# A two-layer graph network on one core: sums of h on GpSimd, aggregates that end bank by bank, and rows put on all partitions by DMA

## The chip, the core and the metric

The kernel runs on one core of a Trainium2 chip. The core has five engines with a queue of instructions each, which run side by side and wait for each other through semaphores: TensorE (PE in the profile, with PEld for its weight loads), VectorE (DVE), ScalarE (ACT), GpSimd (POOL) and SyncE (SP, which here only issues DMAs). Sixteen DMA engines move data between DRAM and the on-chip memory (SBUF). TensorE writes its results to PSUM, eight banks of 128 partitions x 512 f32 values. An instruction of an engine starts only when the one before it in its queue has started, so a wait holds up all that stands behind it.

The metric is the device time of one launch in microseconds, the median of several runs. Before the change it is 3184.61 us (seven runs, 3182.16 to 3187.07).

## What is computed

There are N = 2708 nodes with 1024 features each and a 0/1 matrix adj of 2708 x 2708. Each of two layers normalizes the rows, applies a ReLU, attends over adj and adds the result to x:

```python
# layer 0
h = jnp.maximum(_layernorm(x), 0.0)
f = h @ Wf + bf
g = h @ Wg + bg
e = relu(f @ g.T)
attention = softmax(where(adj > 0, e, -9e15), axis=1)
x = x + attention @ (h @ W + bW)
# layer 1
h = jnp.maximum(_layernorm(x), 0.0)
hW = h @ W1
e = leaky_relu(hW @ a1 + (hW @ a2).T, 0.2)
attention = softmax(where(adj > 0, e, -9e15), axis=1)
x = x + relu(attention @ hW)
```

All is f32.

## The kernel before

**Panels.** The nodes whose attention is computed are cut into five panels p = 0 to 4, with 576, 576, 532, 512 and 512 columns. Within a panel everything is kept transposed: the nodes attended to lie on the partitions, in tiles of 128, and the panel's own nodes lie along the free dimension. There are 20 full tiles, taken as ten pairs q = 0 to 9, and a leftover unit (a tile MONO of 128 nodes and one TINY of 20).

**Seven products.** Each large matrix product is made by Strassen's scheme in Winograd's form: M1 to M7, seven half-size products instead of eight, on sums and differences of the blocks. The sums of the left side (of h, of the weights) are made once, written to DRAM and loaded again for each panel: hs_d holds the blocks of transposed h for the scores, hg_d[layer] the blocks of h for the aggregates, md_d and wt_d the weights' blocks.

**Stages.** First the product M of the weights Wf and Wg is made, while `make_pairs` reads x by pairs, normalizes it, transposes it on TensorE (tile h_ps), makes the sums for the scores on VectorE (`sums`, tile hsT) and stores them to hs_d. Then, for layer 0 and each panel: `project_q` (q), `scores` (ten rounds, one for each pair, each with seven products, tile names sx, sy, sz; the left operands As are loaded from hs_d), a softmax whose steps are spread over later products, `aggregate` (tiles gx, gy, gz, gv; left operands hc loaded from hg_d), and `project` (px, py, pz, pv). For layer 1 and each panel: `weights1` (attention weights from the two scores of each node), `aggregate`, and `project`.

**Order.** A scheduler orders the instructions of each engine and gives the tiles their buffers. The loads on SP's queue keep the order of the program (`load`); stores go through POOL's queue (`store`). Two pools matter: `slots`, 54 buffers of 576 columns, and `strm` (called the stream pool here), 12 buffers of 1024 columns, for all tiles loaded or stored in transit: wg, wf, hsT, As, adj_i, hr, md, hc, hl, w. A load whose buffer isn't free waits on SP, and the loads behind it wait too. Small pieces of work are put into a list by `put` and run between products by `behind`.

**What the change touches.**

- `rows_h` and `sums_h` (the sums of h for layer 0's aggregates). `rows_h` stores the four blocks of each pair as they are to hg_d[0]. After all pairs are made, `sums_h` loads them again, two tiles hr of 512 KB for each pair, makes four operations on VectorE and stores the three places M6 and M7, M3, M5. These pieces run during the scores of panel 0; `sums_until_all` runs what is left ahead of the aggregate's second product.
- `pair_h` does the same from the tiles in SBUF. Before, only layer 1 uses it, on VectorE.
- `accumulate` with `by_k` (the aggregates). The ten pairs are the steps k, and d runs over the four PSUM banks of a product. Before, all steps run k by k with the four banks inside, so the banks end together; then the leftover unit's products (`left_over`, loaded as hl) are added for some products, and the four banks are evicted.
- `spread` puts a column of values (one per partition) on all partitions as a row: a transpose on TensorE for each tile (sp_ps) and a copy out of PSUM. It is used for r in `scores` (rb), for the softmax's maxima (mb), and for z and none in `weights1` (ub, vb). `take_shifts` and `take_weights` run inside the aggregate of the panel before, after its products M3 and M7.

Of the kernel before, what the change touches and what calls it, by code (L numbers as in the profile page):

```python
# [8 lines left out]
FP = mybir.dt.float32  # L9
# [48 lines left out]
def kernel(  # L58
# [69 lines left out]
    def stream(name, shape=(P, D), dt=FP):  # L128
        return strm.tile(list(shape), dt, tag="strm", name=name)
# [7 lines left out]
    def load(o, i):  # L137
        for a, b in in_16(o, i):
            tc.keep_in_program_order(nc.sync.dma_start(a, b))  # L139

    def store(o, i):
        for a, b in in_16(o, i):
            nc.gpsimd.dma_start(a, b)  # L143
# [16 lines left out]
    md_d = dram.tile([P, 7, NH, W], FP, name="md_d")  # L160
    wt_d = [dram.tile([P, 4, NH, W], FP, name=f"wt{l}_d") for l in range(2)]
    mk_d = [dram.tile([P, NQ + 1, 2, width[p]], BF, name=f"mk_d{p}") for p in range(NP)]
    x1_d = [dram.tile([P if t < TINY else NY, D], FP, name=f"x1_d{t}") for t in range(NT)]

    ident = consts.tile([P, P], FP, name="ident")
# [63 lines left out]
    def spread(o, cols):  # L229

        at = 0
        for g in range(0, len(cols), 4):
# [6 lines left out]
            copy(o[:, at:at + w], ps[:, :w])  # L239
            at += w  # L240

    def add(o, a, b):
        nc.vector.tensor_tensor(o, a, b, OP.add)

    def sub(o, a, b):
        nc.vector.tensor_tensor(o, a, b, OP.subtract)
# [42 lines left out]
    def left_h(l, hm, ht):  # L289

        for e in range(2):
            store(hgl_d[l][:, e, :W], hm[e])
            for d in range(NH):
                g = slice(B32 * d, B32 * (d + 1))
                store(hgl_d[l][g, e, W:], ht[e][g, d * P:(d + 1) * P])

    def pair_h(l, q, ha, hb):

        n = P
        on = nc.vector  # L300
# [12 lines left out]
    def rows_h(q, ha, hb):  # L313

        i, j = group_of[q]
        for m, h in ((M1, ha[0]), (M5, ha[1]), (M2, hb[0]), (M4, hb[1])):
            store(hg_d[0][i][:, m, j], h)

    summed = [0]

    def sums_h():

        def fetch(q, two):
            i, j = group_of[q]
            for m in (M1, M2):
                two.append(stream("hr", (P, 2, W)))
                load(two[-1], hg_d[0][i][:, m:m + 2, j])

        def first(q, two):
            (a0, a1), (b0, b1) = ((t[:, 0], t[:, 1]) for t in two)  # L330
            add(b1, a1, b1)
            sub(a1, a0, a1)

        def second(q, two):
            (a0, a1), (b0, b1) = ((t[:, 0], t[:, 1]) for t in two)
            sub(a0, b1, a0)
            sub(b0, b0, a0)
            i, j = group_of[q]
            store(hg_d[0][i][:, M6:M7 + 1, j], two[0])
            store(hg_d[0][i][:, M3, j], b0)  # L340
            store(hg_d[0][i][:, M5, j], b1)
            summed[0] += 1
        for q in range(NQ):
            two = []
            put(1.4, lambda q=q, two=two: first(q, two), lambda q=q, two=two: fetch(q, two))
            put(1.4, lambda q=q, two=two: second(q, two))

    u = consts.tile([P, NC], FP, name="u")
    v = consts.tile([P, NC], FP, name="v")
# [5 lines left out]
    def make_pairs():  # L355
# [6 lines left out]
                load_rows_of(t, xs[q][-1], x)  # L362

        def rows(q):
            left_h(0, *xs[q]) if q == LEFT else rows_h(q, *xs[q])

        def turned(q, k, e):
            t = units[q][k]
# [68 lines left out]
        for i, q in enumerate(todo):  # L437
# [7 lines left out]
            if i == 1:  # L445
                put_dots(todo[0])
                put_dots(todo[1])
        sums_h()

    def make_until(q):  # L450
        while min(q, NQ - 1) not in made:
# [119 lines left out]
        picks.append(t)  # L571


    def accumulate(left, right, K, h, order, then, evict, name, prepare={}, rate=0.0, by_k=False, more={}, room=()):

        acc = {}
        at = {M1: "x", M2: "x", M5: "y", M3: "y", M6: "z", M7: "z", M4: "v" if by_k else "z"}
        for m in order:  # L580
            start = at[m] not in acc
            if start:
                acc[at[m]] = [bank(f"{name}{at[m]}{d}") for d in range(NH)]
            ps = [t[:, :h] for t in acc[at[m]]]
            for k, d in ([(k, d) for k in range(K) for d in range(NH)] if by_k else
                         [(k, d) for d in range(NH) for k in range(K)]):
                nc.tensor.matmul(ps[d], left(m, k, d), right(m, k), start=(start and k == 0),  # L587
                                 stop=(k == K - 1 and m not in more), skip_group_check=True)
                if by_k and d == NH - 1 and k % 3 == 2:
                    behind(rate)  # L590
                if by_k and d == NH - 1 and k == K // 2 and (m, k) in more:
                    more[m, k]()
                if not by_k and k == K - 1:
                    evict[m](d, ps[d])
                    behind(rate, m in room)
            if by_k:
                if m in more:
                    more[m](ps)
                for d in range(NH):
                    evict[m](d, ps[d])  # L600
# [193 lines left out]

    exps, LAG = [0], 2

    def sums_until_all():
        while summed[0] < NQ:
            one()

    def exps_until(n):
        while exps[0] < n:
            one()
# [8 lines left out]
    def aggregate(l, p, S, sm, then={}, rate=3.0):  # L812
# [33 lines left out]
        def left_over(ps, e, s, start=False):  # L846


            two = stream("hl", (P, W + P))
            load(two, hgl_d[l][:, e])  # L850
            for d in range(NH):
                nc.tensor.matmul(ps[d], two[:, d * P:(d + 1) * P], S[MONO][:, s], start=start, stop=False,
                                 skip_group_check=True)
            for d in range(NH):
                g = slice(B32 * d, B32 * d + NY)
                nc.tensor.matmul(ps[d], two[g, W:], S[TINY][g, s], start=False, stop=True, skip_group_check=True)  # L856

        def into_m15():
            ps = [bank(f"gw{d}")[:, :h] for d in range(NH)]
# [219 lines left out]
    def scores(p, B):  # L1079
# [3 lines left out]
        lo, hi = slice(0, h), slice(h, w)  # L1083
        fetch, convert, turn = makers[p]
        rb = slot("rb")
        spread(rb, columns_of(p, r_[:, first_col[p]:]))
        acc = slot("acc")
        S = [None] * NT
        rates = (0.6, 1.0, 0.65, 0.65, 0.65)
# [285 lines left out]
    for p in range(NP):  # L1375
        got["S"], got["acc"] = scores(p, B)
        generated[p] = NQ + 1
        ahead[0] = 2
        S = got["S"]
        hooks = {M1: lambda p=p: take_max(p), M2: lambda p=p: take_softmax(p)}  # L1380
        if p + 1 < NP:
            B = project_q(p + 1, hooks)
        else:
            nc.hold = ("vector",)
            project(0, p - 1, G.pop(p - 1), finish0(p - 1), hooks)
            nc.hold = ()
            scores_before()
        then = {M5: prepare_W} if p == 0 else {}
        if p == 0:
            then[M1] = sums_until_all  # L1390
        if p == NP - 2:
            then[M2] = lambda: first_masks(NP - 1, 0)
            then[M6] = lambda: first_masks(NP - 1, 1)
            then[M7] = lambda: first_masks(NP - 1, 2)
        G[p] = aggregate(0, p, S, got["sm"], then)
        if p == 0:
            flush()
            spread_wa()
# [8 lines left out]
    def weights1(p, z, m, shift):  # L1407
# [2 lines left out]
        ub, vb1, sm = slot("ub"), slot("vb1"), slot("sm")  # L1410

        def spreads():
            spread(ub, columns_of(p, z))
            spread(vb1, columns_of(p, m))
        if p == 0:
# [67 lines left out]
    def take_shifts(p):  # L1483
        flush()
        got["zm"] = shifts1(p)

    def take_weights(p):
        got["P"] = weights1(p, *got["zm"])
# [38 lines left out]
```

## Time and profile before

| | |
|---|---|
| median of seven runs | 3184.61 us (3182.16 to 3187.07) |
| the profiled execution | 3183.64 us, span 3181.8 us, mean granted TensorE clock 0.985 |
| scores of panel 0, first product to last | 209.68 to 434.30 us |
| scores of panel 1, first product to last | 695.50 to 845.05 us |
| one operation of hr on VectorE, 128 x 512 | 0.683 us, 40 of them |
| one load of hr, 512 KB | 20 of them, landing after 7.0 us (median, in the first 520 us) |
| stores of x to hg_d, 256 KB | 40, 0.543 us to issue, landing after 5.1 us |
| DMA over the span | 664.93 MB, 209 GB/s |

The span is the time from the first to the last instruction of the profiled execution; the time of a run is measured around it. A line of a group of instructions names the line of the program, the engine, the operation, the tiles it writes and reads with their shapes, and how many there are; after the bar stand the busy time, the mean duration of one, and the idle time of the engine just before them with what ended it. A line of waits names who waited for whom, and then the total in us, how many times, and the longest. A line of the timeline has the start, the length, the engine, the line and the operation. Instructions that only issue a DMA on SP stand in it as SPq. Line 45 is the helper through which all VectorE and ScalarE instructions go, line 139 is `load` and line 143 is `store`.

### The profile page before, as it was taken

The page shows a single profiled execution, that of the slowest core. Times are in us where ns is not written, and L with a number is a line of the kernel's source. Part 1 is how long each engine was busy: PE and PEld are TensorE (multiplying, and loading weights), DVE is VectorE, ACT ScalarE, POOL GpSimd, SP SyncE. Part 2 cuts the span into 40 slices and gives each one's busy share as a digit, 9 for nine tenths or more (in the row PEclk, how much of TensorE's full clock was granted, in tenths as well). Part 3 has the DMA queues.
Part 4 walks back from the last instruction along what each step waited for, and adds up shares of the span by engine and source line. Part 5 has one row for each costly group of instructions (what it writes and reads, how often), then busy time and mean ns, then how long its engine had stood idle before and what let it go on. Part 6 is the DMA issues. An engine that isn't in the chain of part 4 may idle for free.

```text
span 3181.8 us, 36350 instructions
## 1 busy us (share of the span) xinstructions
PE 3064.4 (96%) x12712; PEld 2268.9 (71%) x12712; DVE 1826.6 (57%) x3770; ACT 447.7 (14%) x788; POOL 421.5 (13%) x644
## 2 busy tenths in 40 slices
PE   8996799999999999999999999997999999999998
PEld 4574577757787588885888886874767758678684
DVE  5775476467651496516973377658574371744612
ACT  3420010010110101101020002103131130211200
POOL 1411101210001110013100101011011020120102
PEclk9998899999999999999999999998999999999999
DMA  6978766789545897458965578596655565565655
GB/s 232 323 247 288 244 229 226 262 240 243 183 143 137 222 252 227 145 151 242 278 193 152 163 216 244 189 289 238 199 163 186 151 197 161 169 199 175 212 160 190
DMA packets 385446, 664.93 MB, mean 209 GB/s; under 512 B 171424, under 2 KB 211904, under 8 KB 385264
## 3 DMA queue, kind: packets, MB, share of 16 engines
q1 hardware_dynamic: 341360, 535.86, 55.5%
q0 software_dynamic: 43904, 126.75, 11.8%
q8 instruction: 101, 1.65, 0.2%
q14 instruction: 81, 0.66, 0.1%
HBM read 547.16 MB, written 115.29 MB: 208 GB/s over the span
## 4 chain that ended last, share of the span: by engine, by line
PE 85%; DMA 5%; DVE 4%; issue 3%; SPq 2%; POOL 1%; ACT 0%; DVEq 0%; POOLq 0%; ACTq 0%
PE gz L587 12%; PE gy L587 11%; PE gx L587 11%; PE sz L1101 6%; PE pz L993 5%; PE gv L587 5%; PE sx L1101 4%; PE px L993 4%; PE py L993 4%; PE sy L1101 4%; PE qz L587 3%; PE M_ps L503 3%; PE qy L587 2%; PE qx L587 2%; SPq L139 2%
## 5 line engine op out<-in xcount | busy, mean ns | idle before, releaser
L1101 PE MATMUL sz<-B,As 128*128 128x288 f32 (+2 forms) x1200 | 295.7, 396 | 12.6 <-DVE st L45 6.9
L1101 PEld LDWEIGHTS sz<-B,As 128*128 128x128 f32 x1200 | 229.8, 192 | 65.1 <-DVE st L45 11.0
L1101 PE MATMUL sx<-B,As 128*128 128x288 f32 (+2 forms) x800 | 211.3, 409 | 43.3 <-DMA As<-hs_d 42.1
L897 POOL TENSOR_TENSOR gT<-gT,rr 128x2304 f32<-128x2304 f32 (+5 forms) x20 | 72.7, 3636 | 1101.9 <-DVE rr L45 998.7
L1101 PEld LDWEIGHTS sx<-B,As 128*128 128x128 f32 x800 | 157.1, 198 | 79.9 <-DMA As<-hs_d 40.7
L1101 PE MATMUL sy<-B,As 128*128 128x288 f32 (+2 forms) x800 | 201.2, 395 | 6.0 <-DMA As<-hs_d 6.0
L587 PE MATMUL gz<-P,hc 128*128 128x288 f32 (+2 forms) x800 | 186.0, 393 | 2.3 <-ACT gT L45 2.3
L587 PE MATMUL gz<-Sa,hc 128*128 128x288 f32 (+2 forms) x800 | 186.0, 393 | 2.3 <-ACT gT L45 2.3
L587 PE MATMUL gx<-P,hc 128*128 128x288 f32 (+2 forms) x800 | 186.4, 395 | 0.0
L587 PE MATMUL gy<-T,hc 128*128 128x288 f32 (+2 forms) x800 | 184.2, 391 | 0.0
L1101 PEld LDWEIGHTS sy<-B,As 128*128 128x128 f32 x800 | 152.6, 191 | 37.9 <-issue 5.5
L587 PEld LDWEIGHTS gz<-Sa,hc 128*128 128x128 f32 x800 | 151.2, 190 | 36.0 <-ACT gT L45 4.4
L587 PEld LDWEIGHTS gx<-P,hc 128*128 128x128 f32 x800 | 153.3, 192 | 32.9 <-issue 1.9
L587 PEld LDWEIGHTS gz<-P,hc 128*128 128x128 f32 x800 | 150.9, 190 | 35.6 <-ACT gT L45 4.4
L587 PEld LDWEIGHTS gy<-T,hc 128*128 128x128 f32 x800 | 152.0, 190 | 30.5
L993 PE MATMUL py<-w,ps 128*128 128x512 f32 x320 | 143.2, 597 | 4.8 <-DMA w<-in_L_gnn_W_dram 4.8
L993 PE MATMUL pz<-w,ps 128*128 128x512 f32 x320 | 143.5, 600 | 0.8 <-DVE pt L45 0.8
L993 PE MATMUL px<-w,gT 128*128 128x512 f32 x320 | 141.9, 596 | 0.7 <-issue 0.7
L143 POOL DMA_DIRECT2D out_dram<-x_res x180 | 89.2, 502 | 265.1 <-DVE x_res L45 258.6
L45 DVE TENSOR_TENSOR gT<-gy,u 128x288 f32<-128x288 f32 (+2 forms) x40 | 14.8, 432 | 183.5 <-PE gy L856 183.5
L993 PEld LDWEIGHTS py<-w,ps 128*128 128x128 f32 x320 | 60.5, 191 | 81.2 <-issue 77.6
L993 PEld LDWEIGHTS pz<-w,ps 128*128 128x128 f32 x320 | 61.0, 192 | 78.6 <-issue 73.0
(316 smaller groups left out, 4970.5 us busy)
## 6 DMA issues: line engine op xcount, KB each, us to landing
hc<-hg_d SPq DMA_DIRECT2D x350, 512.0 KB, 3.9
As<-hs_d SPq DMA_DIRECT2D x150, 512.0 KB, 5.3
w<-wt_d SPq DMA_DIRECT2D x96, 512.0 KB, 5.2
w<-in_L_gnn_W_dram SPq DMA_DIRECT2D x72, 512.0 KB, 4.1
md<-md_d SPq DMA_DIRECT2D x56, 512.0 KB, 5.8
adj_i<-in_adj_dram SPq DMA_DIRECT2D x200, 128.0 KB, 4.9
hs_d<-hsT POOLq DMA_DIRECT2D x40, 512.0 KB, 5.0
As<-hs_d SPq DMA_DIRECT2D x50, 256.0 KB, 4.8
```

The costliest lines, as they stand in the source:

```text
L45: i = f(*a, **k)
L139: tc.keep_in_program_order(nc.sync.dma_start(a, b))
L143: nc.gpsimd.dma_start(a, b)
L503: nc.tensor.matmul(ps, wfT[a][c // NH][:, c % NH, :], wgT[b][c], start=(c == 0), stop=(c == NC - 1))
L587: nc.tensor.matmul(ps[d], left(m, k, d), right(m, k), start=(start and k == 0), stop=(k == K - 1 and m not in more), skip_group_check=True)
L897: nc.gpsimd.tensor_tensor(of(e, s), of(e, s), by(s, k), OP.mult)
L993: nc.tensor.matmul(ps, left[i][m][:, k, :], w_[k], start=(start and k == 0), stop=(k == NH - 1), skip_group_check=True)
L1101: nc.tensor.matmul(ps[:n, :h], lefts[q][:, i % 2, c, :n], B[m][c // 2][:, c % 2, :h], start=(start and c == 0), stop=(c == NH - 1), skip_g ...
```

## The change

Four things change together.

1. The sums of h for layer 0's aggregates are made by `pair_h` on GpSimd when the pair is made, and `rows_h`, `sums_h` and `sums_until_all` go. The raw second block of the first tile is no longer stored.
2. In an aggregate's product the last two steps (TAIL) run bank by bank, and each bank is evicted as it ends. The leftover unit's products come ahead of these two steps.
3. The rows of r for panels 1 to 4 are written to DRAM by DMA, a column's elements one after the other, and loaded back on all partitions.
4. The same for the rows z and none of layer 1's panels 1 to 4.

```diff
+    r_d = [dram.tile([1, WX], FP, name=f"r_d{p}") for p in range(NP)]
+    uv_d = [[dram.tile([1, WX], FP, name=f"uv{k}_d{p}") for k in range(2)] for p in range(NP)]
...
+    def columns_to_row(row, p, col):
+        k = len(pieces[p])
+        nc.gpsimd.dma_start(row[0:1, :W].rearrange("o (i p) -> p (o i)", p=P), col[:, :F])
+        if k > F:
+            n = pieces[p][F][1]
+            nc.gpsimd.dma_start(row[0:1, W:W + n].rearrange("o n -> n o"), col[:n, F:k])
+
+    def row_on_all(o, row, p):
+        load(o[:, :width[p]], row[0:1, :width[p]].to_broadcast([P, width[p]]))
...
     def pair_h(l, q, ha, hb):
         n = P
-        on = nc.vector
+        on = nc.vector if l else nc.gpsimd
...
-    def rows_h(q, ha, hb):
-        i, j = group_of[q]
-        for m, h in ((M1, ha[0]), (M5, ha[1]), (M2, hb[0]), (M4, hb[1])):
-            store(hg_d[0][i][:, m, j], h)
...
-    def sums_h():
-        def fetch(q, two):
-            i, j = group_of[q]
-            for m in (M1, M2):
-                two.append(stream("hr", (P, 2, W)))
-                load(two[-1], hg_d[0][i][:, m:m + 2, j])
-        def first(q, two):
-            (a0, a1), (b0, b1) = ((t[:, 0], t[:, 1]) for t in two)
-            add(b1, a1, b1)
-            sub(a1, a0, a1)
-        def second(q, two):
-            (a0, a1), (b0, b1) = ((t[:, 0], t[:, 1]) for t in two)
-            sub(a0, b1, a0)
-            sub(b0, b0, a0)
-            i, j = group_of[q]
-            store(hg_d[0][i][:, M6:M7 + 1, j], two[0])
-            store(hg_d[0][i][:, M3, j], b0)
-            store(hg_d[0][i][:, M5, j], b1)
-            summed[0] += 1
...
         def rows(q):
-            left_h(0, *xs[q]) if q == LEFT else rows_h(q, *xs[q])
+            left_h(0, *xs[q]) if q == LEFT else pair_h(0, q, *xs[q])
...
+    TAIL = 2
...
-            for k, d in ([(k, d) for k in range(K) for d in range(NH)] if by_k else
-                         [(k, d) for d in range(NH) for k in range(K)]):
-                nc.tensor.matmul(ps[d], left(m, k, d), right(m, k), start=(start and k == 0),
-                                 stop=(k == K - 1 and m not in more), skip_group_check=True)
-                if by_k and d == NH - 1 and k % 3 == 2:
+            whole = K - TAIL
+            for k, d in ([(k, d) for k in range(whole) for d in range(NH)] + [(k, d) for d in range(NH) for k in range(whole, K)]
+                         if by_k else [(k, d) for d in range(NH) for k in range(K)]):
+                nc.tensor.matmul(ps[d], left(m, k, d), right(m, k), start=(start and k == 0), stop=(k == K - 1),
+                                 skip_group_check=True)
+                if by_k and d == NH - 1 and k < whole and (k % 3 == 2 or k == whole - 1):
                     behind(rate)
...
-                if not by_k and k == K - 1:
+                if by_k and d == NH - 1 and k == whole - 1 and m in more:
+                    more[m](ps)
+                if k == K - 1:
                     evict[m](d, ps[d])
-                    behind(rate, m in room)
+                    if not by_k:
+                        behind(rate, m in room)
             if by_k:
-                if m in more:
-                    more[m](ps)
-                for d in range(NH):
-                    evict[m](d, ps[d])
                 behind(rate)
...
         rb = slot("rb")
-        spread(rb, columns_of(p, r_[:, first_col[p]:]))
+        if p == 0:
+            spread(rb, columns_of(p, r_[:, first_col[p]:]))
+        else:
+            row_on_all(rb, r_d[p], p)
...
-        if p == 0:
-            then[M1] = sums_until_all
...
             flush()
+            for s in range(1, NP):
+                columns_to_row(r_d[s], s, r_[:, first_col[s]:])
             spread_wa()
...
         def spreads():
+            if p > 0:
+                for o, row in zip((ub, vb1), uv_d[p]):
+                    row_on_all(o, row, p)
+                return
             spread(ub, columns_of(p, z))
             spread(vb1, columns_of(p, m))
...
         got["zm"] = shifts1(p)
+        for row, col in zip(uv_d[p], got["zm"]):
+            columns_to_row(row, p, col)
```

More of the change, by code (lines that the diff above doesn't have):

```diff
@@ L311, in pair_h @@
         store(hg_d[l][i][:n, M7:M3 + 1, j], g2[:n])
-    def rows_h(q, ha, hb):
-        i, j = group_of[q]
-        for m, h in ((M1, ha[0]), (M5, ha[1]), (M2, hb[0]), (M4, hb[1])):
-            store(hg_d[0][i][:, m, j], h)
-    summed = [0]
-    def sums_h():
-        def fetch(q, two):
-            i, j = group_of[q]
-            for m in (M1, M2):
-                two.append(stream("hr", (P, 2, W)))
-                load(two[-1], hg_d[0][i][:, m:m + 2, j])
-        def first(q, two):
-            (a0, a1), (b0, b1) = ((t[:, 0], t[:, 1]) for t in two)
-            add(b1, a1, b1)
-            sub(a1, a0, a1)
-        def second(q, two):
-            (a0, a1), (b0, b1) = ((t[:, 0], t[:, 1]) for t in two)
-            sub(a0, b1, a0)
-            sub(b0, b0, a0)
-            i, j = group_of[q]
-            store(hg_d[0][i][:, M6:M7 + 1, j], two[0])
-            store(hg_d[0][i][:, M3, j], b0)
-            store(hg_d[0][i][:, M5, j], b1)
-            summed[0] += 1
[L343 to L346, printed above, removed]
     u = consts.tile([P, NC], FP, name="u")
@@ L447, in make_pairs @@
                 put_dots(todo[1])
-        sums_h()
     def make_until(q):
@@ L795 @@
     exps, LAG = [0], 2
-    def sums_until_all():
-        while summed[0] < NQ:
-            one()
     def exps_until(n):
@@ L855, in left_over @@
                 g = slice(B32 * d, B32 * d + NY)
-                nc.tensor.matmul(ps[d], two[g, W:], S[TINY][g, s], start=False, stop=True, skip_group_check=True)
+                nc.tensor.matmul(ps[d], two[g, W:], S[TINY][g, s], start=False, stop=start, skip_group_check=True)
         def into_m15():
```

## The prediction

> **What bounds the kernel now.** I read the page first (busy shares, then the chain that ended last), then TensorE's waits, then busy times by stretch, then SP's queue in the stretch that stood out.
>
> ```profile
> span 3181.8 us, 36350 instructions
> PE 3064.4 (96%) x12712; PEld 2268.9 (71%) x12712; DVE 1826.6 (57%) x3770; ACT 447.7 (14%) x788; POOL 421.5 (13%) x644
> PE 85%; DMA 5%; DVE 4%; issue 3%; SPq 2%; POOL 1%; ACT 0%; DVEq 0%; POOLq 0%; ACTq 0%
> ```
>
> TensorE is busy 96% of the span and has 85% of the chain. So an edit pays where it removes a TensorE wait or TensorE work, and POOL (13%) is free on average. The chain's 5% of DMA (some 160 us) is the largest part that isn't TensorE. TensorE's own waits say where it lies:
>
> ```profile
> PE sx L1101 <- DMA As<-hs_d: 42.1, 7, 11.2
> PE sum_ps L791 <- DVE gT L45: 5.1, 10, 0.5
> PE gz L587 <- ACT gT L45: 4.5, 10, 0.5
> ```
>
> The columns are total, times and longest, in us. The scores' products wait for the tiles As. With the sy and sz products of the same line (6.0 and 4.9) it is 53 us, all between 209 and 434 us, that is in the scores of panel 0. The two others are ten waits each of half a us, one per aggregate. Panel 1 has the same width (576), so its stretch is the measure for panel 0:
>
> ```profile
> 209.00:274.00 65.00, 47.53 (x214) 37.11 (x212) 46.89 (x112) 11.58 (x22) 11.88 (x22) 0.90 0.88 287
> 274.00:434.00 160.00, 124.49 (x467) 91.93 (x468) 87.63 (x170) 0.40 (x1) 21.55 (x36) 0.87 0.83 266
> 760.00:845.00 85.00, 85.00 (x375) 65.68 (x374) 51.10 (x106) 0.40 (x1) 3.25 (x6) 1.00 0.75 224
> ```
>
> After stretch and length come the busy us of PE, PEld, DVE, ACT and POOL, then granted clock, DMA share and GB/s. Panel 1 runs with TensorE full at clock 1.00; panel 0 idles, and its clock falls to 0.87 (each first product after an idle takes about 4.2 us, not 2.1). DVE is at 55% there and DMA moves 266 GB/s, where 321 was seen at 80 to 155 us: neither is the bound. SP's queue is:
>
> ```profile
> 359.37 1.38 SPq L139 DMA_DIRECT2D As<-hs_d  x3
> 361.11 10.48 SPq L139 DMA_DIRECT2D hr<-hg_d  x2
> 373.16 0.33 SPq L139 DMA_DIRECT2D As<-hs_d  x1
> 376.19 6.17 SPq L139 DMA_DIRECT2D adj_i<-in_adj_dram  x8
> ```
>
> Two loads of hr (the rows reloaded for the deferred sums) take 10.48 us, because the second waits for a buffer of the stream pool; the As loads of the next round stand behind it. In 265 to 420 us SP waits 15.7 us for stores of hr and 17.7 us for the mask conversions, whose buffers come late because hr holds two of twelve.
>
> **The change part by part.**
>
> *(a) No reload of h.* It removes 20 loads of 512 KB, 40 DVE operations (40 x 0.683 = 27.3 us) and 30 stores, 21 MB in all, from panel 0's scores. In the changed program SP's order there becomes panel 1's (adj, then As, no hr), and from the sixth round on As waits only for TensorE's reads. Price: panel 0 from the first product of its fourth round (274.17 us) to its last (434.30) took 160.1 us; panel 1's like stretch (737.05 to 845.05) took 108.0. So 52.1 us can go, cold clock included. The first three rounds took 64.5 against 41.6 + 3 x 1.75 of transposes for h = 46.8: another 17.7. There the last pairs are still being made, and the first As tile of the fifth round stands behind the last pair's stores, so I take only 3. Panel 1 was reached with As tiles loaded ahead, panel 0 is not: I give back 3. Taken: -52; ends -69.8 and 0.
>
> *(b) The sums on POOL.* Each of ten pairs gets four 128x512 operations on POOL. POOL's rows of 128x2304 (5.054 us) and 128x1152 (2.622) give 0.19 us + 2.11 ns per element, so 1.27 us each, 5.1 us a pair, 51 us in all. Stores per pair change from four of 0.54 us to three and two of 0.72: +0.9 us of POOL's queue. The cover is 80 to 155 us, four pairs at 15.5 us each: POOL has about 13 issues a pair there, 7 to 8 us, and gets 6. That fits, barely. What is queued behind these operations on POOL is the same pair's stores to hs_d (so the release of the hsT buffers) and stores of md_d; panel 0 needs a pair's hs_d a round or more later. The price on DVE is shown here:
>
> ```profile
> 2309.15 5.05 POOL L897 TENSOR_TENSOR gT<-gT,rr 128x2304 f32<-128x2304 f32 x1 [115.33 <-DVE rr L45]
> 2309.92 4.30 DVE L45 TENSOR_TENSOR z<-f,mcol 128x5 f32<-128x5 f32 x1
> ```
>
> A DVE operation on 128x5 that takes 0.17 us elsewhere took 4.30: it stood until POOL's ended. So POOL's 5.1 us a pair may come out of DVE's time. DVE is 58.4 of 75 us busy there (12.1 of 15.5 a pair); 12.1 + 5.1 is 17.2, over by 1.7 a pair if all of it blocks. TensorE waits for DVE only through the normalized rows, made a pair ahead (the third pair's by 101 us, its transposes at 111 us). Ends: 0, and 4 x 1.7 + 3 x 1.7 for the pairs in panel 0 = +12. Taken: +2.
>
> The Trainium skill (GPSIMD Engine Reference, section Performance versus the Vector engine) speaks against this part: a two-input elementwise operation is about twice as slow on GpSimd as on VectorE, 4497 against 2293 ns at 2048 elements; its 2.6 cycles per element would make 1.11 us of ours, an estimate, and the sum 6 us of POOL less. SBUF — State Buffer, section Who interferes with whom, calls the shared port an exclusive lock, as the 4.30 us show; taken to the letter, all 51 us fall on DVE, and with no slack anywhere the sum would end near -12.
>
> *(c) Banks that end one by one.* The last two pairs run bank by bank (an f32 product with 288 columns takes 0.485 us: 19.40 for 40), so the first bank ends some 2.9 us before the product (3 banks x 2 pairs x 0.485) and its eviction (0.43 us) is over before sum_ps or the next product needs the bank. The waits above go: 5.1 + 4.5 = 9.6. If the evictions came late on a busy DVE, 0. Taken: -9.
>
> *(d) The leftover earlier.* Its load hl moves one hc load ahead on SP and is needed two pairs (3.9 us) earlier. Elsewhere SP runs 10 to 40 us ahead. In the first aggregate it doesn't: TensorE waits 3.35 us for hc at 544 us, and hl, issued at 543.5 behind the rows of W, took 10.33 us on the chain. TensorE would stand about 6 us before hl, and only then run the last pairs. Ends 0 and +6; taken +4.
>
> *(e) Rows of r by DMA.* Panels 1 to 4 lose 18 transposes: 0.73 us where five tiles are spread (694.77 to 695.50), 0.55 where four: 2.6. The rows reach DRAM during panel 0's making; the loads back (rb) stand ahead of adj and As on SP and wait for nothing young. Taken -2.5; ends -2.6 and +4 if rb finds no free slot.
>
> *(f) Rows of z and none by DMA.* The transposes between the sixth and the last product of layer 1's aggregates go: 1.41 + 1.34 + 0.87 + 0.87 = 4.5 (2328.27 to 2329.68 the first). But SP now waits for the rows. Before, the last product's hc loads were issued 40 us ahead (by 2289.8 for 2329.6); now ub and vb stand ahead of them and wait for stores that wait for DVE's none (done 2315.1; with (c) about 1.6 us earlier). A store of 512 single elements is not in the trace. Issue: 0.543 us for 128 pieces, 0.723 for 256, so 1.08 for 512; landing between 2.3 (64 elements of r) and 4.7 (512 pieces of adj_i). Four stores end issuing near 2316.7, land by 2319 to 2321.5; hc follows 0.8 later and lands after 3.9: 2324 to 2326.5, against a need at 2327.1. The narrow panels have about 1.5 us less. So 0 to 1 us late each; with a landing of 9.0 (adj_i's longest) 4 to 5 each. Ends -4.5 and +15; taken -3. Masks and w come behind the same wait, 20 us ahead of need.
>
> For a transfer whose last dimension is strided, the Trainium skill (DMA: Bandwidth & Descriptors, section Rules for kernel authors) has one descriptor per element and advises against it; no run here shows a 4-byte store to DRAM yet.
>
> Sum: -52 + 2 - 9 + 4 - 2.5 - 3 = -60.5. The profiled execution took 3183.6 (span 3181.8), so 3123; the seven runs' median is 1.0 above it: 3124.
>
> **Rivals.**
> 1. *The pace was another's.* SP also waited 17.7 us for mask conversions and 33.6 for TensorE's reads; if these set the round and only hr's share goes (15.7 of 33.4 us, about half), (a) is -26: 3150. For: adj stands ahead of As. Against: panel 1, same order, no wait.
> 2. *Slower: POOL and DVE shut each other out while the pairs are made.* If each POOL operation also waits one DVE operation (1.27 + 0.69 = 1.96 us, 7.8 a pair) and all 78 us land on the path, -52 + 78 - 9 + 4 - 2.5 - 3 = +15: 3200. It decides from 62 us on the path. For: the 4.30 us. Against: DVE has 16.6 us idle in 80 to 155 and TensorE runs full from 72 to 209.
> 3. *Slower: single-element stores.* Were z's rows to land 20 us late in each of four aggregates, with TensorE standing, +80 - 62 gives 3203; it decides from 16 us each. Against: 512 pieces of adj_i land in 4.7.
> 4. *The banks buy nothing* because DVE's in-order queue holds the evictions: 3133, inside the forecast's range.
>
> **How the numbers follow.** Forecast with 4: 0.72, own range 3098 (-69.8 - 9.6 - 2.6 - 4.5) to 3145. Rival 1: 0.15. Rivals 2 and 3: 0.10 together. Within 0.2% (6 us, about what a measurement can tell): 0.03. The range, 3098 to 3158, takes in most of rival 1. Faster 0.86, same 0.03, slower 0.11.
>
> **What would show it.** (a) Panel 0 from its first score product to its last near 165 us, not 224.6, the clock near 1.0 and no As wait after the fifth round. (b) Some forty POOL operations of 1.27 us, DVE operations beside them stretched, transposes at 96 to 153 us not pushed back. (c) No half-us waits of sum_ps and gz. (d) A wait of about 6 us for hl in the first aggregate only. (f) No wait of gv for hc beyond 1 us. Wrong if panel 0 keeps gaps of several us per round, or if it begins later than 215 us.

## The result, and the profile after

The changed kernel takes 3175.6 us (median of 14 runs, 3171.9 to 3181.5), the kernel before 3184.5 (34 runs): the ratio is 0.9972, with a 95% interval of 0.9965 to 0.9979. It is faster, by 9 us, where 60.5 were forecast; the time lies above the forecast's range, 3098 to 3158.

The page of the changed kernel:

```profile
span 3171.7 us, 36132 instructions
PE 3057.4 (96%) x12658; PEld 2266.3 (71%) x12658; DVE 1836.9 (58%) x3721; ACT 447.4 (14%) x779; POOL 476.5 (15%) x682
PE 85%; DVE 6%; DMA 5%; SPq 2%; issue 1%; POOL 1%; ACT 0%; DVEq 0%; POOLq 0%; ACTq 0%
```

The span fell by 10.1 us, and VectorE is 10 us busier although 27 us of its work were taken away; its share of the chain that ended last rose from 4 to 6%. That is the first sign. TensorE's waits in the changed kernel:

```profile
PE gv L567 <- DVE m L45: 17.9, 3, 6.4
PE sx L1079 <- DMA As<-hs_d: 12.9, 3, 7.3
...
PE qx L567 <- ACT m L45: 9.4, 1, 9.4
...
PE gv L567 <- DMA hc<-hg_d: 6.5, 1, 6.5
...
PE h_ps L349 <- ACT M L45: 5.4, 1, 5.4
PE gx L567 <- DMA hc<-hg_d: 5.0, 1, 5.0
...
PE gx L827 <- DMA hl<-hgl_d: 0.5, 1, 0.5
```

The wait for As fell from 42.1 to 12.9 us, and those of sum_ps and gz (5.1 and 4.5) are gone, as forecast. New are the waits of gv (24.4 us, in four aggregates of layer 1) and of qx and h_ps, while the pairs are made. The busy times by stretch, in the columns of the prediction (PE, PEld, DVE, ACT, POOL, clock, DMA share, GB/s): first the making, then panel 0, then panel 1's like stretch.

```profile
140.00:160.00 20.00, 14.62 (x54) 8.12 (x53) 16.68 (x32) 7.40 (x15) 13.69 (x20) 0.92 0.88 335
160.00:180.00 20.00, 15.76 (x58) 11.97 (x58) 17.96 (x30) 8.41 (x17) 13.17 (x19) 0.82 0.99 335
180.00:200.00 20.00, 13.99 (x48) 10.61 (x49) 12.38 (x30) 7.29 (x14) 8.41 (x15) 0.74 0.99 345
...
232.00:297.00 65.00, 53.10 (x226) 41.10 (x226) 47.99 (x112) 11.58 (x22) 25.78 (x34) 0.89 0.97 266
297.00:409.00 112.00, 106.06 (x453) 81.34 (x452) 63.07 (x130) 0.40 (x1) 3.80 (x7) 0.98 0.87 238
735.00:820.00 85.00, 85.00 (x375) 65.64 (x373) 50.92 (x107) 0.40 (x1) 3.25 (x6) 1.00 0.75 225
```

From 140 to 200 us TensorE, full in the kernel before, now idles 15.6 us of 60, and its clock falls to 0.74. Panel 0 in turn runs nearly full from its fourth round, which begins at 293.23 us (106 of 112 us at 0.98, where it was 124 of 160 at 0.87). Where the two traces stand against each other, by TensorE's products:

| boundary | before, us | after, us | difference | in this stage |
|---|---|---|---|---|
| first score product of panel 0 | 209.68 | 232.22 | +22.5 | +22.5 |
| first product after its scores | 434.30 | 409.44 | -24.9 | -47.4 |
| project of panel 0 begins | 646.70 | 623.30 | -23.4 | +1.5 |
| layer 1's first aggregate begins | 2198.32 | 2167.08 | -31.2 | -7.8 |
| layer 1's last aggregate begins | 2987.96 | 2981.03 | -6.9 | +24.3 |
| last product ends | 3169.84 | 3161.65 | -8.2 | -1.3 |
| span | 3181.8 | 3171.7 | -10.1 | -1.9 |

So 47 us were gained in panel 0's scores and 8 in layer 0 behind its first aggregate, and nearly all of it was given back at two places: 22.5 us before panel 0 begins, and 24.3 over four aggregates of layer 1.

### The profile page after: what moved, and what is told of

It is laid out like the page before. It is cut to its first block, busy times and chain, and to the rows that moved or that the text cites. A ratio compares the mean times of both kernels' runs of the same rounds, so it can differ in the third digit from the quotient of the medians.

```text
span 3171.7 us, 36132 instructions
## 1 busy us (share of the span) xinstructions
PE 3057.4 (96%) x12658; PEld 2266.3 (71%) x12658; DVE 1836.9 (58%) x3721; ACT 447.4 (14%) x779; POOL 476.5 (15%) x682
## 4 chain that ended last, share of the span: by engine, by line
PE 85%; DVE 6%; DMA 5%; SPq 2%; issue 1%; POOL 1%; ACT 0%; DVEq 0%; POOLq 0%; ACTq 0%
PE gy L567 12%; PE gx L567 12%; PE gz L567 10%; PE sz L1079 7%; PE gv L567 6%; PE pz L968 6%; PE sx L1079 4%; PE sy L1079 4%; PE py L968 4%; PE px L968 4%; PE qz L567 3%; PE qy L567 2%; PE qx L567 2%; SPq L139 2%; PE M_ps L480 1%
## 5 line engine op out<-in xcount | busy, mean ns | idle before, releaser
L1079 PE MATMUL sx<-B,As 128*128 128x288 f32 (+2 forms) x800 | 203.0, 397 | 14.5 <-DMA As<-hs_d 12.9
L567 PEld LDWEIGHTS gz<-P,hc 128*128 128x128 f32 x800 | 151.3, 190 | 31.6 <-issue 1.8
L968 PE MATMUL px<-w,gT 128*128 128x512 f32 x320 | 141.0, 593 | 0.7 <-issue 0.7
L567 PE MATMUL gv<-P,hc 128*128 128x288 f32 (+2 forms) x400 | 102.4, 419 | 24.4 <-DVE m L45 17.9
L143 POOL DMA_DIRECT2D mk_d<-mask x55 | 36.0, 655 | 550.7 <-DVE mask L45 543.8
```

What stands on the lines that cost most here:

```text
L968: nc.tensor.matmul(ps, left[i][m][:, k, :], w_[k], start=(start and k == 0), stop=(k == NH - 1), skip_group_check=True)
L1079: nc.tensor.matmul(ps[:n, :h], lefts[q][:, i % 2, c, :n], B[m][c // 2][:, c % 2, :h], start=(start and c == 0), stop=(c == NH - 1), skip_g ...
```

## The experiments

Where a time is compared with "before", it is that of the runs of the kernel before on the same chip. Stages are read from the profile of each run, one execution each; scores and aggregates are taken from the start of their first product to the end of their last.

**One part of the change at a time.**

The sums alone:

```diff
 def pair_h(l, q, ha, hb):
-    on = nc.vector
+    on = nc.vector if l else nc.gpsimd
...
-            left_h(0, *xs[q]) if q == LEFT else rows_h(q, *xs[q])
+            left_h(0, *xs[q]) if q == LEFT else pair_h(0, q, *xs[q])
...
-        sums_h()
...
```

> The kernel before, with only the sums of h moved to GpSimd at the making of the pairs. Theory (the terms add: panel 0's scores 47.4 us shorter, the making of the pairs some 21.6 us longer, both as the two traces show): panel 0's scores begin near 231 us and take near 177 us, and the time is 3184.5 - 26 = 3159 us. Rival (the late start comes from something else in the change, such as the stores of r's rows in GpSimd's queue): the scores begin near 210 us, and the time is 3184.5 - 47 = 3137 us.

Measured: 3146.2 us against 3183.1, ratio 0.9887 (0.9873 to 0.9902), so the sums alone gain 37 us, where the whole change gains 9. The time lies between the theory's and the rival's. Panel 0's scores begin at 230.60 us, as the theory has it, but take 168.0 us and not 177. The late start is the sums' own. That the scores are 9 us shorter than in the changed kernel was foreseen by neither side; it points to another part of the change (below).

The bank-by-bank ends alone, with the leftover unit ahead of them:

```diff
-for k, d in ([(k, d) for k in range(K) for d in range(NH)] if by_k else
+whole = K - TAIL
+for k, d in ([(k, d) for k in range(whole) for d in range(NH)] + [(k, d) for d in range(NH) for k in range(whole, K)]
...
```

> The kernel before, with only the aggregates' last two steps bank by bank and the leftover products ahead of them. Theory: each aggregate but the first is 0.9 to 1.2 us shorter (as aggregates 1 to 4 of layer 0 and the last of layer 1 are between the two traces), the ten half-us waits of sum_ps and of gz are gone, the first aggregate gains little: 3184.5 - 9.5 = 3175 us, at worst 3179 if the first aggregate waits 4 us for its leftover. Rival (the shorter aggregates come from the fewer transfers elsewhere): no change, 3184 us.

Measured: 3173.3 us, ratio 0.9970 (0.9959 to 0.9981). Nine aggregates are 0.87 to 1.29 us shorter, 8.5 in all; the first is 3.3 us longer, since its wait for hc goes from 3.3 to 6.7 us and that for hl from 0.3 to 1.2. The theory holds.

The rows of z and none by TensorE again, in the changed kernel:

```diff
-            if p > 0:
-                for o, row in zip((ub, vb1), uv_d[p]):
-                    row_on_all(o, row, p)
-                return
             spread(ub, columns_of(p, z))
...
-        for row, col in zip(uv_d[p], got["zm"]):
-            columns_to_row(row, p, col)
```

> The changed kernel, with z and none put on all partitions by TensorE's transposes as before. Theory (the rows by DMA cost four aggregates of layer 1 6.0 to 6.6 us each in place of a gain, by the two traces, and hide 0.9 us each of the bank-by-bank gain): 3175.6 - 29 = 3147 us, no wait of gv over 1 us. Rival (the new waits of gv come from the bank-by-bank order, whose evictions DVE takes late): gv still waits some 5 us in each, and the time is above 3170 us.

Measured: 3142.4 us, ratio 0.9877 (0.9862 to 0.9891). The four aggregates take 152.7, 150.4, 138.5 and 133.5 us, against 159.6, 157.3, 145.9 and 141.0 with the rows by DMA: 6.9 to 7.5 us each, 28.7 in all, go with part (f). No wait of gv is left.

The sums at the same place, on VectorE:

```diff
-    on = nc.vector if l else nc.gpsimd
+    on = nc.vector
```

> The changed kernel, with the sums of h made at the same place by VectorE (40 operations of 0.68 us, 27 us of VectorE's time) and not by GpSimd. Theory A (VectorE's time is what is short: the operations that stand until GpSimd's end take some 25 us from it, and its own sums take as much): panel 0's scores begin at 228 to 236 us, as with GpSimd, and the time is 3171 to 3180 us. Theory B (what is short is buffers, which GpSimd's slow sums and the stores behind them in its queue hold): the scores begin before 218 us, and the time is 3155 to 3164 us.

Measured: 3165.5 us, ratio 0.9942 (0.9925 to 0.9958); panel 0's scores begin at 220.64 us. That lies between the two theories, and settles neither.

**The rows of r.** The sums and the bank-by-bank ends together, all rows by TensorE:

> The kernel before with the sums on GpSimd and the bank-by-bank ends, and the rows of r and of z and none by TensorE as before. Theory (the rows of r by DMA cost panel 0's scores some 10 us, since their single-element stores tie up the DMA engines: the first experiment's panel 0 took 168.0 us without them, the changed kernel's 177.4 with them): panel 0's scores take 167 to 170 us and the time is 3146.2 - 9.8 = 3136 us. Rival (the two 177 and 178 us and the 168 us are chance of one profile): panel 0 near 177 us and the time 3143 us or more.

Measured: 3140.5 us, ratio 0.9859 (0.9842 to 0.9875); panel 0's scores take 167.8 us. Kernels with r's rows by DMA in this place took 177.4 (the changed kernel), 178.3 (z and none by TensorE), 182.8 (sums on VectorE) and 183.1 us (the run with loads by ScalarE, below), two without them 168.0 and 167.8. The 183.1 us belong to a kernel whose panel 0 is that of the changed one, so the profiles scatter by some 6 us, and the 9.6 us between 177.4 and 167.8 are the least that they show for the rows. The total is 4 us over the expectation: panel 0 starts 1.8 us later than with the sums alone, and the rest of layer 0 behind its first aggregate gains 3.3 us over that run, where the bank-by-bank ends alone had gained 5.9; why wasn't traced. How r's rows act is seen in the DMA issues from 286 to 304 us, of the changed kernel and then of this one (KB each, median us to landing); in the first a store of 512 elements of r is issued at 289.8 us:

```profile
hs_d<-hsT POOLq DMA_DIRECT2D x4, 512.0 KB, 13.5
As<-hs_d SPq DMA_DIRECT2D x3, 512.0 KB, 14.3
adj_i<-in_adj_dram SPq DMA_DIRECT2D x4, 128.0 KB, 17.6
...
r_d<-r POOLq DMA_DIRECT2D x1, 2.0 KB, 13.8
```

```profile
As<-hs_d SPq DMA_DIRECT2D x5, 512.0 KB, 6.5
hs_d<-hsT POOLq DMA_DIRECT2D x4, 512.0 KB, 7.1
adj_i<-in_adj_dram SPq DMA_DIRECT2D x8, 128.0 KB, 6.4
```

A store of 2 KB in 4-byte pieces takes 13.8 us to land, and the groups of 128 to 512 KB shown take about twice as long as without it or more. In that stretch 203 GB/s are moved with it and 342 without, at a DMA share near 1 in both. The store also stands in GpSimd's queue (3.4 us of waiting for r ahead of 289.8 us, with three hs_d stores behind it). How much of the 10 us each of the two makes was not told apart.

The same with the sums on VectorE:

> The same with the sums of h on VectorE. Theory (half of the late start of panel 0 comes from VectorE's time, which is short with either engine, and half from GpSimd's queue and the buffers it holds): panel 0's scores begin near 219 us, and the time is 3 to 9 us under the run with the sums on GpSimd, 3127 to 3133 us. Rival (without the rows of r, VectorE's sums fit into its idle time): they begin before 214 us, and the time is under 3125 us.

Measured: 3123.7 us, ratio 0.9807 (0.9793 to 0.9822); the scores begin at 218.60 us. The theory holds for the start; the gain over GpSimd's sums is larger, 17 us, and the time is where the rival had it.

**What the sums on GpSimd cost.** To part VectorE's shut-out from the buffers that the sums hold, the kernel before was given additions on GpSimd that nothing needs:

```diff
+    idle = consts.tile([P, W], FP, name="idle")
+    def idle_sums(q):
+        c = col_of[units[q][1]]
+        for _ in range(4):
+            nc.gpsimd.tensor_tensor(idle, ones[:, :1].to_broadcast([P, W]), r_[:, c:c + 1].to_broadcast([P, W]), OP.add)
```

> The kernel before, and beside it four additions of 128x512 on GpSimd for each pair, ones plus a column of r into a tile that nobody reads, issued behind the pair's second dot product: they hold no buffer of a load, but they shut VectorE out and stand in GpSimd's queue ahead of stores. Theory A (the shut-out and the queue make the late start): panel 0's scores begin at 222 us or later, and the time is 3195 us or more. Theory B (the buffers that the sums hold make it): panel 0's scores begin before 214 us and the time is under 3188 us. Between: each has its share, in that proportion.

Measured: 3204.3 us, ratio 1.0060 (1.0045 to 1.0075); the scores begin at 227.21 us, 17.5 later than before. Then, to part the shut-out from the time in GpSimd's queue, fills in place of the additions:

```diff
-        for _ in range(4):
-            nc.gpsimd.tensor_tensor(idle, ones[:, :1].to_broadcast([P, W]), r_[:, c:c + 1].to_broadcast([P, W]), OP.add)
+        nc.vector.tensor_copy(idle[:, :1], r_[:, c:c + 1])
+        for _ in range(9):
+            nc.gpsimd.memset(idle, 0.0)
```

> The idle sums of the run before last, but each pair's four additions replaced by nine fills of 128x512 on GpSimd (0.54 us each in the trace, 4.9 us a pair against 5.1) that read nothing, and so much the same time in GpSimd's queue ahead of the stores. Theory A (VectorE is shut out by GpSimd's two-input operations): no VectorE operation is stretched to 4 us by a fill, panel 0's scores begin before 214 us, and the time is 3180 to 3190 us. Theory B (the stores that stand behind GpSimd's work come late): panel 0's scores begin at 222 us or later, as with the additions (227.2), and the time is 3195 us or more.

Measured: 3183.1 us, ratio 0.9999 (0.9990 to 1.0009); the scores begin at 210.60 us. The instruction groups from 60 to 235 us, with the additions (the first three lines) and with the fills (the last three):

```profile
L45 DVE SCALAR_TENSOR_TENSOR junk<-x,vb 128x512 bf16<-128x512 f32 x34 | 28.0, 824 | 5.4 <-ACT x L45 4.4
L45 DVE BATCH_NORM_STATS2 bn<-x 128x6 f32<-128x512 f32 x30 | 20.4, 684 | 0.0
...
L325 POOL TENSOR_TENSOR idle<-ones,r 128x512 f32<-128x512 f32 x28 | 31.6, 1128 | 7.8 <-DVE r L45 7.0
```

```profile
L45 DVE SCALAR_TENSOR_TENSOR junk<-x,vb 128x512 bf16<-128x512 f32 x36 | 24.7, 686 | 6.3 <-ACT x L45 5.3
L45 DVE BATCH_NORM_STATS2 bn<-x 128x6 f32<-128x512 f32 x34 | 22.9, 684 | 0.0
...
L326 POOL MEMSET idle<- 128x512 f32 x72 | 39.2, 544 | 13.4 <-DVE idle L45 10.5 <-DMA x<-in_x_dram 2.1
```

39.2 us of fills cost 0.9 us of the start; 31.6 us of additions, which hold no buffer, cost 17.5. So it is neither the queue nor the buffers that makes the 17.5: VectorE is shut out, and of these two kinds only by the operations of GpSimd that read. The sums themselves cost 20.9 us of the start; what makes the 3.4 us between was not told apart.

Last, the run with the sums on VectorE, each pair's sums of h behind its sums for the scores:

```diff
...
         def last(q):
             sums(q)
+            if q != LEFT:
+                rows(q)
...
```

> The run with the sums on VectorE and all rows by TensorE (3123.7 us, panel 0's scores from 218.6 us), with each pair's sums of h behind its sums for the scores. Theory (what is left of the late start, 218.6 against 209.7 us before the change, is VectorE's order: the sums of h stand ahead of work that TensorE waits for): the scores begin before 215 us, and the time is 3115 to 3121 us. Rival (it is VectorE's time as a whole, or the buffers held): the scores begin at 217 us or later, and the time is 3122 us or more.

Measured: 3116.3 us, ratio 0.9787 (0.9771 to 0.9803); the scores begin at 207.82 us and take 168.4. Nothing of the late start is left: on VectorE the 27 us of sums fit beside TensorE's work once they stand behind what TensorE waits for. GpSimd's sums in this later place were not run.

**What the rows of z and none cost.** The stretch in the changed kernel, VectorE and then TensorE (start, length):

```profile
2282.03 0.16 DVE L45 SCALAR_TENSOR_TENSOR none<-f,m 128x5 f32<-128x5 f32 x1
2299.98 0.82 DVE L45 SCALAR_TENSOR_TENSOR P<-ub,f,P 128x576 f32<-128x576 f32 x1 [17.79 <-ACT P L45]
2300.71 1.54 DVE L45 TENSOR_TENSOR m<-gw,m 128x288 f32<-128x288 f32 x4
```

```profile
2286.78 0.77 PE L831 MATMUL gw<-P,hl 20*128 20x288 f32 x8
2287.48 8.03 PE L567 MATMUL gz<-P,hc 128*128 128x288 f32 x32
2301.22 10.95 PE L567 MATMUL gv<-P,hc 128*128 128x288 f32 x32 [5.71 <-DVE m L45]
```

VectorE stands 17.8 us ahead of the first product with ub, and behind it stand the evictions of gw, whose products were done by 2287.5 us and whose banks gv needs; they ran at 2300.71 us. In the kernel before they ran as soon as gw's products were done, ahead of the copies of ub:

```profile
2320.33 1.55 DVE L45 TENSOR_TENSOR m<-gw,m 128x288 f32<-128x288 f32 x4 [5.22 <-PE gw L856]
```

The rows' stores took 8.3 to 9.3 us to land here, with next to nothing else on the DMA engines. First, the loads of the rows were given to ScalarE's queue:

```diff
-                    row_on_all(o, row, p)
+                    nc.scalar.dma_start(o[:, :width[p]], row[0:1, :width[p]].to_broadcast([P, width[p]]))
```

> The changed kernel, with the loads of z's and none's rows issued by ScalarE's queue, so that SP's loads of hc behind them do not wait. Theory (what holds gv is VectorE's order: its first product with ub stands in its queue ahead of the four evictions of gw and waits for the rows): gv still waits 5 us or more for m in each of four aggregates of layer 1, which stay at 157 to 161 us for the first two, and the time is within 5 us of the changed kernel's. Rival (SP's standing 40 us for the rows, so that hc comes late): the waits go, the first two aggregates take under 154 us, and the time falls by 20 us or more.

Measured: 3178.0 us, ratio 0.9980 (0.9971 to 0.9989); gv waits 26.4 us in four for m. It agrees with the theory, but the edit did less than it meant: SP still stood 35.4 us for ub in this stretch, at the loads behind.

Next, three cures at once: r's stores held behind the first aggregate, the rows' loads behind all of the last product's hc, and the first product with ub held behind the evictions (the sums on VectorE here too):

```diff
-        nc.gpsimd.dma_start(row[0:1, :W].rearrange("o (i p) -> p (o i)", p=P), col[:, :F])
+        tc.keep_in_program_order(nc.gpsimd.dma_start(row[0:1, :W].rearrange("o (i p) -> p (o i)", p=P), col[:, :F]))
...
-                hc[m, i] = stream("hc", (P, 2, W))
+                for i2 in range(len(groups)) if (l, m) == (1, M4) else [i]:
...
+                    if i == 0:
+                        tc.keep_in_program_order(o)
```

> The changed kernel with the sums on VectorE, the stores of r's rows held behind the first aggregate's work on GpSimd, the loads of z's and none's rows placed behind all loads of hc of the aggregate's last product, and the first product with ub held behind the evictions of gz. Against the run with the sums on VectorE and all rows by TensorE (3123.7 us). Theory (what the rows cost is DMA engines tied up at a bad time, hc's loads behind the rows on SP and VectorE's order, and all three are now gone): panel 0's scores near 168 us as there, the four aggregates of layer 1 shorter than there by 1.4, 1.3, 0.9 and 0.9 us, panels 1 to 4 by 2.4 in all: 3123.7 - 7 = 3117 us. Rival (the rows still come too late for the next weights, or their stores slow hc's loads): the aggregates are not shorter, and the time is 3121 to 3135 us.

Measured: 3173.2 us, ratio 0.9963 (0.9948 to 0.9978), far off the theory. Panel 0's scores are right (166.2 us), but the project after the first aggregate is 8.1 us longer than in the changed kernel, 6.1 of it a wait for w. r's stores, issued from 573 us on, now meet the loads that stand ahead of w on SP: those of x, 64 KB each, land after 9.7 us and not 4.4 as in the run with all rows by TensorE, and w is issued 15.6 us after the project's start and not 1.4. The four aggregates of layer 1 are 33 us longer than in that run, and gv waits as before:

```profile
PE gv L567 <- DVE m L45: 28.1, 4, 7.6
```

Here the loads of hc were issued by 2254 us, 27 us before gv could begin (gz ends at 2281.2), so SP's queue is out of it. Only the product of the first tile had been held; those of the next tiles were put ahead of the evictions in its place. Then, on the best kernel and with r by TensorE, all products with ub held (the diff is against the run before):

```diff
-                    if i == 0:
+                    if p > 0:
                         tc.keep_in_program_order(o)
```

> The run with the sums on VectorE behind the sums for the scores (3116.3 us), with the rows of z and none by DMA again, their loads behind all loads of hc of the aggregate's last product, and now all products with ub held in the program's order on VectorE, behind the evictions of gw and gz. Theory (what costs the aggregates of layer 1 their 6 us is VectorE's order alone: in the run with mended rows hc was loaded 30 us ahead, and gv still waited 28.1 us in four for m, because only the first of the products with ub was held): gv waits under 1 us in each, the four aggregates take 151.3, 149.0, 137.6 and 132.6 us, which is 1.4, 1.3, 0.9 and 0.9 less than with transposes, and the time is 3112 us. Rival (the rows are too late in any order): gv or the next aggregate's products wait, or the projects between them grow, and the time is 3117 us or more.

Measured: 3116.9 us, ratio 0.9794 (0.9780 to 0.9807). No wait of gv is left, and the four aggregates take 150.7, 148.8, 137.6 and 132.6 us, 5.3 less than in the run with the sums behind, as the theory has it. In the time this doesn't show: 3116.9 against 3116.3, with intervals that overlap, where the theory had 3112. What VectorE's order did to (f) is settled; that the rows by DMA are then worth having is not.

## Why the prediction was right in sign and wrong in size

| part | forecast | measured | from |
|---|---|---|---|
| (a) no reload of h | -52 | -56.8 | panel 0's scores, 224.8 to 168.0, sums alone |
| (b) sums on GpSimd | +2 | +20.9 | their start, 209.68 to 230.60, sums alone |
| (c) banks end one by one | -9 | -9.4 | nine aggregates, 8.5, and about 0.9 in the first |
| (d) leftover earlier | +4 | +2.5 | first aggregate +1.6, with -0.9 of (c) taken out |
| (e) rows of r | -2.5 | +7 | -2.6 at four panel starts, +9.6 in panel 0 |
| (f) rows of z and none | -3 | +28.7 | four aggregates, changed kernel less third run |
| sum | -60.5 | -7.1 | the spans differ by 10.1 |

The 3 us that the sum lacks lie between the layers (1.3) and after the last product (1.9); no part was traced to them.

- *(a) and (c)* were right, mechanism and size. Panel 1 as the measure for panel 0, and the first rounds counted apart, held: with the sums alone panel 0 took 108.0 us from its fourth round on, exactly as panel 1 (160.1 before), and 59.8 for the first three (64.5 before). Rival 1 (half of it another's pace) and rival 4 (banks for nothing) fall.
- *(d)* came near in size by another wait than the one named. The 6 us were to be a wait for hl; in the changed kernel TensorE waited 0.5 us for hl and 5.0 for hc ahead of it (0.3 and 3.3 before).
- *(b)* is the first step that failed: "The cover is 80 to 155 us ... That fits, barely", with +12 as its end. The mechanism was named and its row was right (4.30 us), but I charged VectorE 5.1 us a pair once, over 75 us, and set it against VectorE's idle time on average. What counts is which operation is caught. GpSimd's sums follow each other, one operation of VectorE is held through three of them, and what stands behind the caught operation is what TensorE needs next (VectorE, then GpSimd):

```profile
153.20 4.41 DVE L45 SCALAR_TENSOR_TENSOR junk<-x,vb 128x512 bf16<-128x512 f32 x1
157.54 0.08 DVE L45 DVE_READ_ACCUMULATOR junk<-x,vb 128x1 f32 x1
157.54 0.68 DVE L45 BATCH_NORM_STATS2 bn<-x 128x6 f32<-128x512 f32 x1
```

```profile
153.34 1.28 POOL L316 TENSOR_TENSOR g<-x 128x512 f32<-128x512 f32 x1
154.58 1.26 POOL L318 TENSOR_TENSOR g<-x 128x512 f32<-128x512 f32 x1
155.80 1.26 POOL L317 TENSOR_TENSOR g<-g,x 128x512 f32<-128x512 f32 x1
```

  The first operation, 0.69 us elsewhere, lasted from 153.20 to 157.61, while three of GpSimd's sums ran from 153.34 to 157.06. Behind it stood the statistics (mv), for these ScalarE's square root, behind that in ScalarE's queue the eviction of M, and for its bank TensorE's next transposes (ScalarE, then TensorE):

```profile
159.09 0.29 ACT L45 ACTIVATE rs<-mv,eps 128x1 f32<-128x1 f32 x1 [8.44 <-DVE mv L45]
159.30 0.57 ACT L45 COPY M<-M_ps 128x512 f32<-128x512 f32 x1
```

```profile
159.91 1.12 PE L349 MATMUL h_ps<-ident,x 128*128 128x128 f32 x4 [5.38 <-ACT M L45]
```

  So 5.4 us of TensorE's time go through two other engines' queues to one caught operation. TensorE's other long wait there, 9.4 us before qx at 186.01, also ends on an eviction that stood in ScalarE's queue behind VectorE's statistics, after an operation of 1.35 us had been caught for 4.47. From 60 to 235 us such stretches add 24 us to VectorE: dot products 9.7, r 5.9, those of wg 3.1, hT 3.1, the rest 2. Rival 2 was this mechanism, at 78 us if all landed on the path; about a quarter of that did.

  The Trainium skill (SBUF — State Buffer, section Who interferes with whom) says more than I weighed: a VectorE instruction with two inputs in SBUF contends with a GpSimd instruction that reads SBUF, not with one that only writes it, and one with at most one input in SBUF, outside VectorE's two-port modes, doesn't contend. The runs agree on each point: the dot products are stretched from 0.69 to 0.82 us in the mean by additions and not by fills, the statistics (one input) stay at 0.684 beside both. The prediction's own line from that page, that with no slack the sum ends near -12, came nearest to the result, but by chance: it charged 51 us to (b), of which 20.9 came, and (e) and (f) brought the rest.
- *(e)* failed in what it left out. I asked when r's rows arrive and what rb waits for; the stores themselves were priced by their issue alone. They had a price for everything beside them: +9.6 us or more where two of them met panel 0's loads. The skill's advice against a last dimension that is strided (DMA: Bandwidth & Descriptors, section Rules for kernel authors) stood in the prediction only under (f), and the runs bear it out under (e).
- *(f)* is the largest failure: "0 to 1 us late each", with +15 as its end. Two terms were off. Landing was put at 2.3 to 4.7 us, and took 9.0 in the median (8.3 to 10.2); only the issue was dearer in the forecast, 1.08 us for 512 elements against 0.8. And the late rows were followed into one queue only, SP's and hc; there one of gv's four waits in the changed kernel ended (6.5 us). They were also waited for in VectorE's queue, where the scheduler had put the first product with ub ahead of the evictions that free gv's banks. The last two runs show that this order made the waits: with hc 27 us ahead they stayed, with the order held as well they went. The order held without hc ahead was not run. Rival 3 named the late stores, with the price that decides at 16 us each; 7 us each came.
- *The balance.* 86 of 100 for faster was right. The range was not: its upper end took in rival 1 and little of rivals 2 and 3, which came in part and together, some 60 us between them with (e).

The version that beats both kernels leaves out (e) and (f), makes the sums on VectorE behind the sums for the scores, and keeps (a), (c) and (d): 3116.3 us.

## What to carry to other kernels

Work given to GpSimd is not free because GpSimd is idle: ask whether its instruction reads SBUF while VectorE has two-input work on the path, and charge that work the whole length of each GpSimd instruction, at the place where it is caught. When a value arrives later by another way, follow the wait into every in-order queue that holds an instruction which reads it, the computing engines' first, and ask what stands behind it there. A transfer of single elements is priced by what it does to the transfers around it, not by its issue.

## What the hardware showed that was not expected

- A VectorE operation with two inputs in SBUF is held for as long as GpSimd's additions last (0.69 us became 4.41; one on 128x1 went from 0.21 to 4.17), while beside 72 fills of GpSimd, 39.2 us, the same dot products kept 0.69 us, and one-input statistics stayed at 0.684 us beside either.
- Stores to DRAM of 20 to 512 single 4-byte elements took 9.0 us to land in the median for z and none (8.3 to 9.3 where next to nothing else moved) and 10.8 for r, 13.8 at most, among other transfers. Beside the slowest of them, the groups of 128 to 512 KB shown above landed 6 to 11 us later than without it.
